# First block's maxima by pairs of key chunks over eight PSUM banks, and one-row reciprocals spread through HBM, in a kernel of attention and a non-local block

## The chip, the cores and the metric

The kernel runs on one NeuronCore of one Trainium2 chip. The metric is the device time of one execution in microseconds. Three runs of the kernel before gave 4115.18, 4115.48 and 4115.97 us; the median is 4115.48.

The engines are PE (TensorE, matrix products into PSUM), DVE (VectorE), ACT (ScalarE), POOL (GpSimd) and SP (SyncE, which here only issues DMAs). [...]

## The reference

The input x is 2 x 256 x 64 x 64. The first layer is self-attention over the 4096 pixels with 8 heads of 32 channels, the second a non-local block with pooled keys. Cut to what is computed:

```python
# layer 0
qkv = einsum('oc,bchw->bohw', w_qkv, x)
q, k, v = split(qkv, 3, axis=1)            # each b, 8 heads, 32, 4096
scores = einsum('bhdi,bhdj->bhij', q, k) / sqrt(32)
attn = softmax(scores, axis=-1)
out = einsum('bhij,bhdj->bhdi', attn, v)
x = einsum('oc,bchw->bohw', w_proj, out) + x
# layer 1
g = maxpool2(conv1x1(x, g_w, g_b))
theta = conv1x1(x[:, :64], theta_w, theta_b)
phi = maxpool2(conv1x1(x[:, 64:], phi_w, phi_b))
y = softmax(theta^T phi) @ g
x = batchnorm(conv1x1(y, W_w, W_b)) + x
```

Softmax subtracts the row's maximum before the exponential, and divides by the row's sum.

## The kernel before

Heads are taken four at a time; two batches with two such quads give four quads `n` = 0 to 3. In a quad the 4096 queries are eight blocks `i` of 512, so 32 blocks are attended one after another. Within a block the loop runs over 32 key tiles `j` of 128 keys. One step of it (L464 to L495) does, on PE, for each pair of heads, the subtraction of the row maxima (`subtract`, a small bfloat16 product, on even `j`) and the scores (`score`); on ACT the exponentials `p` (L481); on PE the product of the previous step's exponentials with v (`weigh`, into `w`); on DVE the addition of `w` into `num` (L401); and on POOL the sums of the exponentials for the denominator (`add`): the first pair of heads by an addition (L414), the second by an accumulating DMA of two tiles (L422).

The odd steps don't compute scores anew: keys of an odd chunk are stored as differences to the even chunk before (`kd` for the first four chunks of 512 keys, `last_kd` for the last four), and their product is added into the bank that still holds the even scores.

The row maxima of a block are needed before its attention, so they are found one block ahead, by the generator `maxima`, which the loop moves on by a step at a time (`advance(maxes)`). A step takes two heads. `plain` makes the product of 128 queries with 512 keys and takes its maximum over the keys on DVE (L249). `pair` finds the maximum over two chunks: the product with the differences, cut at zero by ACT (`over`, L256), and then the product with the even chunk, which DVE adds to `over` and reduces at once (L259). In the blocks after the first, heads 2 and 3 go mostly by `pair`, heads 0 and 1 by `plain`. All products of the maxima are in `scratch` tiles (four banks of pool `ps_m`); scores take tiles of two banks (pool `ps_s`, two of them). `scratch` also holds `w`, `den`, and k, q and v products during attention. Banks of a pool are given out in turn, and an allocation waits until the bank's last user is done.

Before attention starts, the opening loop (L701 to L708) makes k and v of quad 0, chunk by chunk, and q of two blocks; there the k, q and v products are in `ps_s`. Each is copied out by ACT (L187, L204). Between the halves of these products the maxima of the first block move on, all by `plain`: 128 products of 512 keys, 128 reductions. Then (L709 to L713) what remains of the first block is done, its maxima are negated into `neg` (L311), split into three bfloat16 terms on POOL, and the second block's maxima are begun.

A block's denominator is taken during the next block, by the generator `normalize`: at step 2 the last accumulating DMA, at step 6 the product with ones into `den` and ACT's copy of it into `r` (128x512; every head's row of 512 sums stands there 32 times), then eight reciprocals of 64 columns each, one a step (L451 to L455), and at the end the multiplication by POOL into `y` (L456). `issue_after(reduced.ins)` puts a reciprocal behind the maxima's last reduction on DVE. The two last blocks of the batches are normalized in `project`, halfway.

Loads of x are issued by SP (L88). In attention one tile holds x, so a load is issued as soon as the last product of the tile's previous content is done; steps 11, 19 and 27 make the next q, k and v from it.

The order on each engine is set by a scheduler that works from priorities and its own estimate of times, within the order of the data; each engine runs its instructions in that fixed order, and SP its DMA issues too.

Of the kernel before, what the change touches and what calls it, by code (L numbers as in the profile page):

```python
# [9 lines left out]
F32 = mybir.dt.float32  # L10
BF16 = mybir.dt.bfloat16
AF = mybir.ActivationFunctionType
# [5 lines left out]
HEADS, D = 8, 32  # L18
QH = 4
# [16 lines left out]
def conv_attention(  # L36
# [23 lines left out]


    ps_s = ctx.enter_context(tc.tile_pool(name="ps_s", bufs=2, space=bass.MemoryType.PSUM))
    ps_m = ctx.enter_context(tc.tile_pool(name="ps_m", bufs=4, space=bass.MemoryType.PSUM))

    def scores(name):
        return ps_s.tile([P, 2, NB], F32, tag="s", name=name)

    def scratch(name):
        return ps_m.tile([P, NB], F32, tag="m", name=name)
# [91 lines left out]
    def make(what, n, i):  # L161
        b, qd = QUAD[n]
        if held.get("x") != (b, i):
            held["x"] = (b, i)
            name = f"x_{what}_{n}_{i}"
            held["t"] = load_x(
                b, i, xs.tile([P, NC, NB], F32, tag="x", name=name) if attending else single(name)
            )
        xc = held["t"]
        name = f"{what}_{b}_{qd}_{i}"  # L170

        pq = scratch(name) if attending else scores(name)[:, 0, :]
        if what == "v":
            if i == 0:
                v[n] = qkv.tile([P, NJ, QH, D], F32, tag="v", name=f"v_{n}")
            for j in range(NB // P):
                for c in range(NC):
                    nc.tensor.matmul(  # L178
                        pq[:, bass.ts(j, P)],
                        xc[:, c, bass.ts(j, P)],  # L180
                        wv_sb[:, c, bass.ts(qd, P)],
                        start=(c == 0),
                        stop=(c == NC - 1),
                    )
                if j % 2 == 1:
                    yield
            nc.scalar.copy(v[n][:, bass.ts(i, NB // P)].rearrange("p j h d -> p (j h d)"), pq)  # L187
            return
        for c in range(NC):
            nc.tensor.matmul(  # L190
                pq,
                wqk_sb[:, c, qd, 0 if what == "q" else 1, :],
                xc[:, c, :],
                start=(c == 0),
                stop=(c == NC - 1),
            )
            yield
        if what == "q":
            to = q[n, i] = qkv.tile([P, NB], F32, tag="q", name=f"q_{n}_{i}", bufs=3)
        else:  # L200
            if i == 0:
                k[n] = qkv.tile([P, N], F32, tag="k", name=f"k_{n}")
            to = k[n][:, bass.ts(i, NB)]
        nc.scalar.copy(to, pq)  # L204
        if what == "k" and i == NI // 2 - 1:
            kd[n] = qkv.tile([P, NI // 4, NB], F32, tag="kd", name=f"kd_{n}")
            differences(n, 0, kd[n])

# [23 lines left out]
    part = const.tile([P, NB // P, QH, NI], F32, name="part")  # L232
    nc.vector.memset(part, LEAST)

    def product(n, i, g, h, keys):
        ps = scratch(f"ps_{n}_{i}_{g}_{h}")
        nc.tensor.matmul(  # L237
            ps,
            q[n, i][bass.ts(h, D), bass.ts(g, P)],
            keys[bass.ts(h, D), :],  # L240
            start=True,
            stop=True,
        )
        return ps

    def plain(n, i, g, h, j):
        nonlocal reduced
        ps = product(n, i, g, h, k[n][:, bass.ts(j, NB)])
        reduced = nc.vector.tensor_reduce(part[:, g, h, j : j + 1], ps, AX.X, ALU.max)  # L249

    def pair(n, i, g, h, jp):

        nonlocal reduced, cut
        ps = product(n, i, g, h, (kd[n] if jp < NI // 4 else last_kd)[:, jp % (NI // 4), :])
        over = work.tile([P, NB], F32, tag="over", name=f"over_{n}_{i}_{g}_{h}")
        cut = nc.scalar.activation(over, ps, AF.Relu)  # L256
        yield
        ps = product(n, i, g, h, k[n][:, bass.ts(2 * jp, NB)])
        reduced = nc.vector.tensor_tensor_reduce(  # L259
            out=ps,  # L260
            in0=ps,
            in1=over,
            scale=1.0,
            scalar=LEAST,
            op0=ALU.add,
            op1=ALU.max,
            accum_out=part[:, g, h, 2 * jp : 2 * jp + 1],
        )
        yield

    G = NB // P

    def of_head(n, i, h):

        chunks = 0 if h < 2 else NI // 2 if i == 0 else NI
        pairs = [(g, jp) for jp in range(chunks // 2) for g in range(G)]
        plains = [(g, j) for g in range(G) for j in range(chunks, NI)]
        if h == 3:  # L280
            if not plains:
                g, jp = pairs.pop()
                plains = [(g, 2 * jp), (g, 2 * jp + 1)]
            plain(n, i, plains[0][0], h, plains[0][1])
            plains = plains[1:]
            yield
        for x in pairs:
            yield from pair(n, i, x[0], h, x[1])
        for x in plains:
            plain(n, i, x[0], h, x[1])  # L290
            yield

    def maxima(n, i):
        if (n, i) == (0, 0):

            for j in range(NI):
                for g in range(G):
                    for two in (1, 0):
                        for h in (2 * two, 2 * two + 1):
                            plain(n, i, g, h, j)  # L300
                        yield
        else:
            heads = [of_head(n, i, h) for h in range(QH)]
            for step in range(G * NI):

                for two in ((2, 3) if step % 2 == 0 else (3, 2)), (0, 1):
                    for h in two:
                        next(heads[h])
                    yield
        neg = work.tile([P, NB // P, QH], F32, tag="neg", name=f"neg_{n}_{i}")  # L310
        nc.vector.tensor_reduce(neg, part, AX.X, ALU.max, negate=True)  # L311
        rows.append(negate(f"{n}_{i}", len(rows), neg))
        if i == 0:
            nc.vector.memset(part[:, :, 2:, :], LEAST)


# [9 lines left out]
    def advance(steps, n=1):  # L326
        for _ in range(n):
            next(steps, None)
# [12 lines left out]
    def attend(b, y):  # L341
# [82 lines left out]
        def normalize(blk):  # L424
            whole = [1, 2]
            if (blk.qd, blk.i) != (QUADS - 1, NI - 1):
                with tc.issue_after(added.ins):
                    nc.gpsimd.dma_start(out=blk.sums[1], in_=blk.sums[2], accum_op=ALU.add)
                whole = [1]
                yield  # L430
            den = scratch(f"den_{blk.name}")
            mine = [
                [blk.sums[0], *blk.last],
                [blk.sums[n][:, j] for j in range(2) for n in whole],
            ]
            for n in range(max(map(len, mine))):
                for h in range(QH):
                    those = mine[h // 2]
                    if n < len(those):
                        nc.tensor.matmul(  # L440
                            den[bass.ts(h, D), :],
                            ones[:, :D],
                            those[n][:, h % 2, :],
                            start=(n == 0),
                            stop=(n == len(those) - 1),
                        )
            r = work.tile([P, NB], F32, tag="r", name=f"r_{blk.name}", bufs=1)
            nc.scalar.copy(r, den)
            yield

            for c in range(8):  # L451
                cols = bass.ts(c, NB // 8)
                with tc.issue_after(reduced.ins):
                    nc.vector.reciprocal(r[:, cols], r[:, cols])
                yield  # L455
            nc.gpsimd.tensor_mul(y[:, blk.qd, bass.ts(blk.i, NB)], blk.num, r)  # L456

        waiting, normal = None, iter(())
        for qd in range(QUADS):
            for i in range(NI):  # L460
# [3 lines left out]
                for j in range(NJ):  # L464
# [24 lines left out]
                        advance(normal)  # L489
                    if j % 2 == 0:  # L490
                        make_rows()
                        if (i, j) == (0, NJ // 4):
                            differences(blk.n, 1, last_kd)
                    elif j % 8 == 3 and j > 8 and items:
                        advance(make(*items.pop(0)), 9)  # L495
# [202 lines left out]
    attending = False  # L698


    for i in range(NI + 1):  # L701
        items = [(what, 0, i) for what in "kqv" if i < (2 if what == "q" else NI)]
        for item in items:
            pieces = make(*item)
            for n in range(3):
                advance(pieces)
                if i > 0 and item[0] != "q" and n < 2:
                    advance(maxes, 2)  # L708
    advance(maxes, 8)  # L709
    advance(maxes)  # L710
    make_rows()
# [61 lines left out]
```

## Time and profile before

| What | Value |
|---|---|
| median of three runs | 4115.48 us |
| profiled execution, its own time | 4114.88 us |
| its span, first to last instruction | 4113.1 us |
| mean granted PE clock | 0.996 |
| opening stage, up to the first exponential | 125 us |
| attention of batch 0, one block, 463.00 to 570.55 us | 107.55 us |
| in that block, busy: DVE, ACT, POOL | 87.41, 80.83, 87.98 us |
| in that block, DMA share of 16 engines | 0.77 |
| one reciprocal of 128x64 on DVE | 543 ns |
| one maximum over a product, 128x512 | 686 ns, 0.61 us from one to the next |
| one cut of a product by ACT, 128x512 | 597 ns |
| one pair reduction on DVE, 128x512, and the read of its accumulator | 699 and 142 ns |

The page of the profile gives busy shares over the whole span; they mix an opening stage, two stages of attention of about 1725 us each, and two of projection and non-local block. So the stages are read one by one below. PE's busy time is modelled (its matmuls are pipelined), so the distance from one group of matmuls to the next says more than its busy share.

### The profile page before, as it was taken

How to read it: one execution, taken by the hardware profiler on the slowest of the kernel's cores; microseconds unless marked ns; L12 is line 12 of the kernel's file. 1: busy time of each engine (PE TensorE's matmuls, PEld its weight loads, DVE VectorE, ACT ScalarE, POOL GpSimd, SP SyncE). 2: the span in 40 equal slices, each digit the busy share in tenths (PEclk: the TensorE clock that was granted, in tenths of full speed). 3: DMA queues.
4: the chain of work that ended last, by engine and by line, in shares of the span. 5: the costliest groups of instructions: out<-in, count | busy, mean ns of one | idle time of the engine just before them, and what ended most of it. 6: DMA issues, size and time to landing. Idle time of an engine off the chain costs nothing.

```text
span 4113.1 us, 75018 instructions
## 1 busy us (share of the span) xinstructions
PE 4085.4 (99%) x29712; PEld 1539.1 (37%) x29712; DVE 3075.7 (75%) x5661; ACT 2647.4 (64%) x3264; POOL 2920.1 (71%) x1855
## 2 busy tenths in 40 slices
PE   9999999999999999999999999999999999999998
PEld 4433333333333333333333333333333333333333
DVE  7788888888888888884448888888888888883444
ACT  1677777776777777761137777777677777777111
POOL 0677887777877887780448878877788888889143
PEclk9899999999999999999999999999999999999999
DMA  1477777777777777781008777777777777778300
GB/s 58 102 157 158 158 157 157 155 163 156 156 157 156 161 157 162 162 171 45 21 21 165 158 161 160 155 157 158 158 163 157 156 159 157 151 155 172 80 16 26
DMA packets 98735, 560.70 MB, mean 136 GB/s; under 512 B 9552, under 2 KB 11344, under 8 KB 37200
## 3 DMA queue, kind: packets, MB, share of 16 engines
q0 software_dynamic: 68832, 501.25, 60.3%
q1 hardware_dynamic: 28288, 53.48, 4.5%
q8 instruction: 232, 3.80, 0.4%
q10 hardware_dynamic: 1264, 1.19, 0.1%
q14 instruction: 119, 0.97, 0.1%
HBM read 46.28 MB, written 8.39 MB: 13 GB/s over the span
## 4 chain that ended last, share of the span: by engine, by line
PE 97%; DVE 2%; DMA 0%; POOL 0%; issue 0%; ACT 0%; DVEq 0%; ACTq 0%; POOLq 0%
PE ps L237 31%; PE w L390 25%; PE s L366 18%; PE y L638 5%; PE s L378 5%; PE v L178 2%; PE k L190 2%; PE q L190 2%; PE den L440 1%; PE g L564 1%; DVE r L652 1%; PE f L606 1%; PE proj L510 1%; PE f L670 1%; PE tp L548 0%; PE tp L544 0%
## 5 line engine op out<-in xcount | busy, mean ns | idle before, releaser
L414 POOL TENSOR_TENSOR p<-p,p 128x1024 f32<-128x1024 f32 x960 | 2338.7, 2436 | 610.5 <-ACT p L481 490.8
L237 PE MATMUL ps<-k,q 32*128 32x512 f32 x6360 | 2206.5, 621 | 0.9 <-ACT over L256 0.6
L481 ACT ACTIVATE p<-s 128x1024 f32<-128x1024 f32 x2048 | 1990.7, 1024 | 114.7 <-PE ps L237 47.1
L249 DVE TENSOR_REDUCE part<-ps 128x1 f32<-128x512 f32 x2264 | 1453.1, 686 | 117.3 <-PE ps L237 74.7
L390 PE MATMUL w<-p,v 128*32 128x512 f32 x8192 | 1091.9, 605 | 0.0
L366 PE MATMUL s<-q,k 32*128 32x512 f32 x4096 | 1031.0, 595 | 0.0
L259 DVE CUSTOM_DVE_ANT_0 ps<-ps,over 128x512 f32<-128x512 f32 x916 | 639.8, 699 | 484.7 <-PE ps L237 255.0
L237 PEld LDWEIGHTS ps<-k,q 32*128 32x128 f32 x6360 | 830.6, 184 | 312.4 <-DVE num L401 103.3
L256 ACT ACTIVATE over<-ps 128x512 f32<-128x512 f32 x916 | 547.2, 597 | 615.0 <-PE ps L237 607.6
L401 DVE TENSOR_TENSOR num<-num,w 128x512 f32<-128x512 f32 x992 | 661.9, 667 | 80.3 <-PE w L390 77.7
L237 PE MATMUL ps<-kd,q 32*128 32x512 f32 x992 | 560.8, 645 | 0.0
L366 PE MATMUL s<-q,last_kd 32*128 32x512 f32 x2048 | 511.5, 614 | 0.0
L366 PE MATMUL s<-q,kd 32*128 32x512 f32 x2048 | 510.7, 615 | 0.6 <-ACT p L481 0.6
L237 PE MATMUL ps<-last_kd,q 32*128 32x512 f32 x840 | 470.6, 640 | 0.0
L390 PEld LDWEIGHTS w<-p,v 128*32 128x32 f32 x8192 | 161.5, 108 | 777.5 <-ACT over L256 685.6
L422 POOL DMA_DIRECT2D p<-p x448 | 388.8, 868 | 57.3 <-ACT p L481 53.5
L378 PE MATMUL s<-rows,ones_b 32*128 32x512 bf16 x2048 | 395.3, 380 | 0.2 <-ACT p L481 0.2
L366 PEld LDWEIGHTS s<-q,k 32*128 32x128 f32 x4096 | 366.7, 184 | 5.7 <-issue 1.4
L378 PEld LDWEIGHTS <-ones_b 32*128 32x128 bf16 x2048 | 128.6, 91 | 499.3 <-PE ps L237 209.6
L366 PEld LDWEIGHTS s<-q,kd 32*128 32x128 f32 x2048 | 174.3, 184 | 221.8 <-ACT p L481 192.5
L366 PEld LDWEIGHTS s<-q,last_kd 32*128 32x128 f32 x2048 | 173.9, 184 | 205.9 <-ACT p L481 186.7
L638 PE MATMUL y<-p,kv 128*128 128x512 f32 x512 | 240.0, 608 | 3.7 <-DVE r L652 3.7
(99 smaller groups left out, 2309.1 us busy)
## 6 DMA issues: line engine op xcount, KB each, us to landing
p<-p POOLq DMA_DIRECT2D x478, 1024.0 KB, 7.4
x_k<-in_x_dram SPq DMA_DIRECT2D x32, 512.0 KB, 4.1
x_q<-in_x_dram SPq DMA_DIRECT2D x30, 512.0 KB, 5.7
x_res<-in_x_dram SPq DMA_DIRECT2D x16, 512.0 KB, 8.5
out_dram<-z SPq DMA_DIRECT2D x16, 512.0 KB, 2.7
x_v<-in_x_dram SPq DMA_DIRECT2D x6, 512.0 KB, 4.4
wqk_sb<-in_wqk_dram ACTq DMA_DIRECT2D x1, 512.0 KB, 5.5
g<-in_gw_dram SPq DMA_DIRECT2D x2, 256.0 KB, 9.6
```

The source lines that it names most:

```text
L237: nc.tensor.matmul(ps, q[n, i][bass.ts(h, D), bass.ts(g, P)], keys[bass.ts(h, D), :], start=True, stop=True,)
L249: reduced = nc.vector.tensor_reduce(part[:, g, h, j : j + 1], ps, AX.X, ALU.max)
L256: cut = nc.scalar.activation(over, ps, AF.Relu)
L259: reduced = nc.vector.tensor_tensor_reduce(out=ps, in0=ps, in1=over, scale=1.0, scalar=LEAST, op0=ALU.add, op1=ALU.max, accum_out=part[:, ...
L366: nc.tensor.matmul(s[:, t, :], kj[bass.ts(h, D), :], q[blk.n, blk.i][bass.ts(h, D), :], start=False, stop=True, skip_group_check=j % 2 == 1,)
L378: nc.tensor.matmul(s[:, t, :], ones_b[bass.ts(h, D), :], rows[blk.rows][bass.ts(h, D), :], start=True, stop=False,)
L390: nc.tensor.matmul(w[bass.ts(h, D), :], v[blk.n][:, keys(j), h, :], p[h // 2][:, h % 2, :], start=True, stop=True,)
L401: nc.vector.tensor_add(blk.num, blk.num, w)
L414: added = nc.gpsimd.tensor_add(blk.sums[0], blk.sums[0], p[0])
L422: nc.gpsimd.dma_start(out=blk.sums[n], in_=two, accum_op=ALU.add)
L481: nc.scalar.activation(p[pair], s, AF.Exp, scale=scale)
L638: nc.tensor.matmul(acc[i][o], wg[:, 2 * t + j, bass.ts(o, P)], p[:, j, :], **edge)
```

## The change

Three things are changed together.

First block: its maxima are taken by pairs of chunks for all four heads. `first_block` makes, for a pair of chunks and a group of 128 queries, four products with the differences (two in scratch banks, two in the two banks of a scores tile), four cuts by ACT into a tile of the exponentials' pool, four products with the even chunk and four pair reductions. One step of the generator has four heads now. The opening loop has one round less and takes one such step between the halves of a k or v product from chunk 2 on, and the k, q and v products there go to scratch banks. The differences of quad 0 are made for each pair of chunks as soon as both are there, by a POOL operation of 128x512 each. As the first block leaves the odd slots of `part` at the least value, they are not reset for quad 0.

Reciprocals: the rows of `r` for the four heads, one for each, are written to HBM by a DMA, read back laid out over 128 partitions of 16 values (`few`), inverted in one operation on DVE, written to HBM, and copied by four DMAs to the 32 partitions of each head in `r`. The block normalized in the projection has one reciprocal of 128x512 instead.

Waits: five steps lie between the read back and the reciprocal in the written order, and five between the copies and the multiplication.

```diff
+    spare = ctx.enter_context(
+        tc.tile_pool(name="spare", bufs=2, space=bass.MemoryType.DRAM)
+    )
...
-        pq = scratch(name) if attending else scores(name)[:, 0, :]
+        pq = scratch(name)
...
-        if what == "k" and i == NI // 2 - 1:
+        if what == "k" and i % 2 == 1 and n == 0:
+            if i == 1:
+                kd[n] = qkv.tile([P, NI // 4, NB], F32, tag="kd", name=f"kd_{n}")
+            two = k[n][:, bass.ts(i // 2, 2 * NB)]
+            nc.gpsimd.tensor_sub(
+                (kd[n] if i < NI // 2 else last_kd)[:, i // 2 % (NI // 4), :],
+                two[:, NB:],
+                two[:, :NB],
+            )
+        elif what == "k" and i == NI // 2 - 1:
...
-    def product(n, i, g, h, keys):
-        ps = scratch(f"ps_{n}_{i}_{g}_{h}")
+    def product(n, i, g, h, keys, ps=None):
+        if ps is None:
+            ps = scratch(f"ps_{n}_{i}_{g}_{h}")
...
+    def first_block():
+        for jp in range(NI // 2):
+            for g in range(G):
+                over = double(f"over_{jp}_{g}").rearrange("p a b n -> p (a b) n")
+                for what in range(2):
+                    if what == 0:
+                        keys = (kd[0] if jp < NI // 4 else last_kd)[:, jp % (NI // 4), :]
+                    else:
+                        keys = k[0][:, bass.ts(2 * jp, NB)]
+                    s = scores(f"ps_{jp}_{g}_{what}")
+                    ps = [
+                        product(0, 0, g, h, keys, s[:, h - 2, :] if h >= 2 else None)
+                        for h in range(QH)
+                    ]
+                    for h in range(QH):
+                        if what == 0:
+                            nc.scalar.activation(over[:, h, :], ps[h], AF.Relu)
+                        else:
+                            joint(ps[h], over[:, h, :], g, h, jp)
+                    yield
...
-        chunks = 0 if h < 2 else NI // 2 if i == 0 else NI
+        chunks = 0 if h < 2 else NI // 2 if i == 0 and n > 0 else NI
...
         if (n, i) == (0, 0):
-            for j in range(NI):
-                for g in range(G):
-                    for two in (1, 0):
-                        for h in (2 * two, 2 * two + 1):
-                            plain(n, i, g, h, j)
-                        yield
+            yield from first_block()
...
-        if i == 0:
+        if i == 0 and n > 0:
             nc.vector.memset(part[:, :, 2:, :], LEAST)
...
-            for c in range(8):
-                cols = bass.ts(c, NB // 8)
+            if (blk.qd, blk.i) == (QUADS - 1, NI - 1):
+                nc.vector.reciprocal(r, r)
+            else:
+                flat = [spare.tile([QH, NB], F32, tag=f"flat{a}", name=f"flat{a}_{blk.name}") for a in range(2)]
+                few = work.tile([P, NB // D], F32, tag="few", name=f"few_{blk.name}")
+                nc.sync.dma_start(out=flat[0], in_=r[::D, :])
+                nc.sync.dma_start(out=few, in_=flat[0].rearrange("h (c e) -> (h c) e", c=D))
+                for _ in range(5):
+                    yield
                 with tc.issue_after(reduced.ins):
-                    nc.vector.reciprocal(r[:, cols], r[:, cols])
-                yield
+                    nc.vector.reciprocal(few, few)
+                nc.sync.dma_start(out=flat[1].rearrange("h (c e) -> (h c) e", c=D), in_=few)
+                for h in range(QH):
+                    nc.sync.dma_start(
+                        out=r[bass.ts(h, D), :], in_=flat[1][h : h + 1, :].broadcast_to([D, NB])
+                    )
+                for _ in range(5):
+                    yield
             nc.gpsimd.tensor_mul(y[:, blk.qd, bass.ts(blk.i, NB)], blk.num, r)
...
-                        if (i, j) == (0, NJ // 4):
+                        if (i, j) == (0, NJ // 4) and blk.n > 0:
                             differences(blk.n, 1, last_kd)
...
-    for i in range(NI + 1):
+    for i in range(NI):
         items = [(what, 0, i) for what in "kqv" if i < (2 if what == "q" else NI)]
         for item in items:
             pieces = make(*item)
             for n in range(3):
                 advance(pieces)
-                if i > 0 and item[0] != "q" and n < 2:
-                    advance(maxes, 2)
+                if i > 1 and item[0] != "q" and n < 2:
+                    advance(maxes)
```

`joint` is the pair reduction of before (L259 to L268) as a function of its own; `pair` calls it.

More of the change, by code (lines that the diff above doesn't have):

```diff
@@ L251, in pair @@
     def pair(n, i, g, h, jp):
-        nonlocal reduced, cut
+        nonlocal cut
         ps = product(n, i, g, h, (kd[n] if jp < NI // 4 else last_kd)[:, jp % (NI // 4), :])
@@ L257, in pair, with joint @@
         yield
-        ps = product(n, i, g, h, k[n][:, bass.ts(2 * jp, NB)])
+        joint(product(n, i, g, h, k[n][:, bass.ts(2 * jp, NB)]), over, g, h, jp)
+        yield
+    def joint(ps, over, g, h, jp):
+        nonlocal reduced
         reduced = nc.vector.tensor_tensor_reduce(
@@ L449, in normalize @@
             yield
-            for c in range(8):
-                cols = bass.ts(c, NB // 8)
-                with tc.issue_after(reduced.ins):
-                    nc.vector.reciprocal(r[:, cols], r[:, cols])
-                yield
+            if (blk.qd, blk.i) == (QUADS - 1, NI - 1):
[7 more added lines that the diff above has]
+                    yield
+                with tc.issue_after(reduced.ins):
+                    nc.vector.reciprocal(few, few)
[5 more added lines that the diff above has]
+                for _ in range(5):
+                    yield
             nc.gpsimd.tensor_mul(y[:, blk.qd, bass.ts(blk.i, NB)], blk.num, r)
```

## The prediction

> **What bounds the kernel now.** I read the page first, then the times of the matmuls `w` of one block of the attention loop, then the opening 125 us by windows, then POOL and the DMA queues.
>
> ```profile
> span 4113.1 us, 75018 instructions
> PE 4085.4 (99%) x29712; PEld 1539.1 (37%) x29712; DVE 3075.7 (75%) x5661; ACT 2647.4 (64%) x3264; POOL 2920.1 (71%) x1855
> PEclk9899999999999999999999999999999999999999
> PE 97%; DVE 2%; DMA 0%; POOL 0%; issue 0%; ACT 0%; DVEq 0%; ACTq 0%; POOLq 0%
> ```
>
> PE carries 97% of the chain of waits, but ends of matmuls are modelled, so "99% busy" doesn't say that PE never waits. The weigh matmuls `w` (L390), one group per key tile, are a clock for the loop. These are from the timeline of PE, in one block (start, length):
>
> ```profile
> 467.64 1.06 PE L390 MATMUL w<-p,v 128*32 128x512 f32 x8
> 471.22 1.07 PE L390 MATMUL w<-p,v 128*32 128x512 f32 x8
> 474.18 1.06 PE L390 MATMUL w<-p,v 128*32 128x512 f32 x8
> 477.72 1.07 PE L390 MATMUL w<-p,v 128*32 128x512 f32 x8
> 480.71 1.07 PE L390 MATMUL w<-p,v 128*32 128x512 f32 x8
> ...
> 498.83 1.06 PE L390 MATMUL w<-p,v 128*32 128x512 f32 x8
> 501.82 1.07 PE L390 MATMUL w<-p,v 128*32 128x512 f32 x8
> 504.96 1.06 PE L390 MATMUL w<-p,v 128*32 128x512 f32 x8
> 507.95 1.06 PE L390 MATMUL w<-p,v 128*32 128x512 f32 x8
> ...
> L454 DVE RECIPROCAL r<-r x256: 494/543/554, 253.9 to 3837.9; 128x64 f32<-128x64 f32 x128
> ```
>
> The reader is to see that the late steps take 2.99 and 3.14 us in turn, while steps with a reciprocal (key tiles 7 to 14) take 3.58, 2.96, 3.54, 2.99, then (after the step that also makes q) 3.40, 3.14, 3.40. So four of the eight 543 ns reciprocals delay PE by 0.41 to 0.45 us: DVE runs the addition into `num` after the reciprocal, and the scratch bank that it frees comes late. DVE is the bound of these steps, hidden under "PE".
>
> The opening stage, by windows (us, busy and count of PE, PEld, DVE, ACT, POOL, granted clock, DMA):
>
> ```profile
> 40.00:60.00 20.00, 20.00 (x94) 9.71 (x93) 16.22 (x28) 1.76 (x3) 2.35 (x1) 1.00 0.00 1
> 100.00:120.00 20.00, 20.00 (x57) 12.83 (x54) 15.93 (x29) 2.39 (x4) 1.22 (x5) 0.53 0.00 0
> ...
> 94.08 15.83 DVE L249 TENSOR_REDUCE part<-ps 128x1 f32<-128x512 f32 x24 [0.96 <-PE ps L237]
> ```
>
> DVE is the bound (81%), ACT is nearly empty, and PE's clock is halved near 101 to 125 us. The first block's maxima end with the reduction into `neg` at 109.94 us and attention starts near 121.5.
>
> [...]one halving lasts from about 2138.8 to 2142.3 us[...]. [...]reciprocal and addition into `num` always follow in the order written. [...]
>
> **The change, part by part.**
>
> (a) Reciprocals. Removed: 8 x 543 ns a block on DVE. Added in the place of the sixth: one of 128x16. From the rows 128x64 (543 ns) and 128x512 (3358 ns, L652) the slope is 6.28 ns an element and the intercept 141, so 0.24 us. Against 3.13 and 2.99 the excess over steps 7 to 14 is 0.45 - 0.03 + 0.42 + 0 + 0 + 0.41 + 0 + 0.41 = 1.66 us. A reciprocal of 0.54 costs 0.41, so 0.13 of it is covered; 0.24 costs 0.11. Gain 1.55 us a block. Thirty blocks are normalized inside the loop; the last of these lies in a block without maxima, whose steps show no excess. 29 x 1.55 = 45 us. Next late is PE's own 2.99 and 3.13, and I take these whole because the late steps of the same blocks, with the same other work, already run at that pace. Bounds: 22 us, if only half goes, to 48 us. The two blocks normalized in the projection get one reciprocal of 3.36 us for eight of 0.54: 1 us less, under 28 us of projection matmuls: nothing.
>
> (b) Seven DMAs more a block on SP: the lay-out (4 x 2 KB), the read back (128 x 64 B), the write (128 x 64 B), and four copies of 64 KB. `r` is copied by ACT at 250.73 us in the second block; with 0.37 us per SP issue and 3 to 4 us to landing (x loads of 512 KB take a median 4.1 to 5.7 with these queues; I take 3 for small ones), the row values are in `few` by 259, and the reciprocal stands at 271.9: 12 us of cover. SP's order puts the load of x for q ahead of the lay-out, and that for k (free when q's matmuls end at 268.6) ahead of the write, so no load is late. DMA bytes grow by 0.3 MB a block against 17. Nothing.
>
> (c) The multiply on POOL moves. In the instruction order of the new kernel it stands two additions earlier, straight behind the addition of key tile 13 and ahead of the accumulating DMA of tile 12. Before:
>
> ```profile
> 274.51 2.36 POOL L414 TENSOR_TENSOR p<-p,p 128x1024 f32<-128x1024 f32 x1 [0.82 <-ACT p L481]
> 276.82 0.86 POOL L422 DMA_DIRECT2D p<-p  x1
> 277.88 2.35 POOL L414 TENSOR_TENSOR p<-p,p 128x1024 f32<-128x1024 f32 x1 [0.20 <-ACT p L481]
> 280.20 1.27 POOL L456 TENSOR_TENSOR y<-num,r 128x512 f32<-128x512 f32 x1
> ...
> p<-p POOLq DMA_DIRECT2D x478, 1024.0 KB, 7.4
> x_k<-in_x_dram SPq DMA_DIRECT2D x32, 512.0 KB, 4.1
> ```
>
> So POOL can want `r` from 276.9. The chain: reciprocal done at 272.1, write lands at 275.2 (3 us), four issues of 0.37 to 276.7, last copy lands near 279.3. POOL waits about 2.4 us; behind it stand the accumulating DMA of 12 and the additions. That DMA starts at 281, not 276.8, and lands by 288.5. Its double buffer is next written by the exponential of tile 18, second pair, at 290.4; two reciprocals fewer bring that to 289.6. So it just fits: 1 us to spare, and POOL's idle time (0.94 us in two steps, 20%) takes up the rest. I take nothing, except in the last block where POOL is the bound (92% busy at 3700 to 3800): +2 us once. Bounds: 0 to 3 us in each of 29 blocks.
>
> (d) First block. DVE: 128 reductions of 0.61 us become 64 pair reductions of about 0.76 (0.70 and the read of the accumulator), 78 us to 49; ACT gains 64 cuts of 0.60, 38 us. But the banks decide. k and v products now use the four scratch banks in turn with the maxima: one for the product, two for the differences' heads 0 and 1, two for the even chunk's. The fifth falls on the bank of the k or v product itself, whose copy stands on ACT behind the four cuts. Each of the 12 passes (k and v of chunks 2 to 7) is thus a closed chain: bank free to PE 0.15 (a cut ends at 904.89, the next weigh starts at 905.03), four products 1.07, first half of the next k or v 1.06, four products 1.07, to ACT 0.08, four cuts 2.40, copy 0.59: 6.42 us, though PE has only 4.2 and DVE 3.0 of work. Passes start when chunk 1 is done, 20.9 us (chunk 0 to 14.6, then about 2.1 each for k, q, v): 20.9 + 12 x 6.42 = 98. The last four pairs are bound by DVE: 4 x 3.05 and 3 us to fill and drain, 113. Against 109.94: 3 us later, at full clock.
>
> (e) The clock. Count a matmul record of 128 rows as one and one of 32 rows as a quarter, 0.43 us each (four k records take 1.91). From 40 to 90 us the groups give 138 products, 20 k, 64 v of a quarter's length: (34.5 + 20 + 16) x 0.43 / 50 = 61% of the array, clock full. After 97.7 us only two products stand in every 1.22 us (two reductions): 35%, and the clock was halved. In the new chain the average is 3.44 / 6.42 = 54%, but in bunches: [...] at half clock the 3.2 us of PE in the chain double and the pass takes 9.6. Its dense stretch, first half, four products, second half, is 3.2 us, 6.4 at half clock[...]. I take half of the passes slow: 6 x 3.2 = 19 us. Bounds: 0, and all 12 with the tail, 41 us.
>
> Sum, on the profiled execution of 4114.88 us (span 4113.1 and 1.8 around it; 0.6 below the median): -45 + 3 + 19 + 2 = -21, which is 4094; against the median 4094.5. I say 4094.
>
> **Rivals.** A change within 0.2%, 8 us, is no change that can be told.
> - Forecast, clock swings in the opening: 4094, own range 4082 to 4105. Chance 0.45.
> - The clock stays full, or the bank chain is looser than I read it: -45 + 3 + 2, 4075. For it: the average of 54% is near the 61% that held. Against: the bunches. 0.15.
> - The clock locks at half through the opening: -45 + 3 + 41 + 2, 4116. For it: once halved before, it stayed so for 24 us of sparse work. Against: the denser stretch. 0.20.
> - Slower: the multiply waits too long for `r`. Place: POOL, behind tile 13. Price: each us beyond about 1 more than I reckon stalls an exponential in 29 blocks; slower than before from 0.9 us a block (21 + 8 over 29), and at 2 us 4152. For it: 64 B writes and a busy DMA (77%). Against: 1 us of room and POOL's idle time. 0.12.
> - Half of (a) only, because another release is late in these steps: 4116. Against: the late steps. 0.08.
>
> Faster: 0.44 + 0.15 + 0.04 + 0.02 = 0.65. Within 0.2%: 0.11 of the locked clock, 0.04 of the last case, 0.01: 0.16. Slower: 0.12 + 0.05 + 0.02 = 0.19. The range runs from the second case less its error in (a), 4070, to the locked clock with a little of POOL, 4124; of the chances about 0.13 lie outside.
>
> **What would show it.** Steps 7 to 14 at 2.99 and 3.13; in the opening, the maxima's products waiting for ACT's copy once a pass of 6.4 us, and the end of `neg`'s reduction near 132 us (113 at full clock, 155 if locked); granted clock under 1 between 25 and 110 us; POOL's multiply idle by 2 to 3 us before it, released by a DMA of `r`; no wait of ACT's exponentials for p<-p. I am wrong if passes take under 5.5 us, if steps 7 to 14 keep an excess over 0.5 us a block, or if exponentials wait for DMA.

## The result and the profile after

The changed kernel takes 4075.32 us (median of four runs, 4069.38 to 4079.79); the kernel before, run beside it, 4115.33. The ratio is 0.9902, with a 95% interval of 0.9885 to 0.9919: about 40 us, or 1%, less. The profiled execution took 4069.38 us, with a span of 4067.6; it is the fastest of the four, so its trace shows the small side of what the change loses.

The page of the changed kernel:

```profile
span 4067.6 us, 75418 instructions
PE 4022.1 (99%) x29712; PEld 1496.0 (37%) x29712; DVE 2951.2 (73%) x5436; ACT 2674.9 (66%) x3328; POOL 2925.4 (72%) x1857
PE 89%; DMA 6%; DVE 2%; POOL 1%; ACT 1%; issue 1%; SPq 0%; POOLq 0%; DVEq 0%; ACTq 0%
```

The time fell, and yet DMA now has 6% of the chain of waits, where it had 0%. So something was gained and something else was newly lost. The two have to be read in their stages.

**The opening.** The timeline of PE for two passes (start, length; a k or v product comes in two halves, with four products of the maxima, eight records, behind each):

```profile
20.16 1.14 PE L249 MATMUL ps<-kd,q 32*128 32x512 f32 x8
21.23 1.12 PE L192 MATMUL k<-x_k,wqk_sb 128*128 128x512 f32 x2
22.29 1.14 PE L249 MATMUL ps<-k,q 32*128 32x512 f32 x8
23.36 1.16 PE L180 MATMUL v<-wv_sb,x_k 128*128 128x128 f32 x8
24.45 1.14 PE L249 MATMUL ps<-kd,q 32*128 32x512 f32 x8
...
28.73 1.14 PE L249 MATMUL ps<-kd,q 32*128 32x512 f32 x8
```

From 20.16 to 24.45 and from there to 28.73: a pass takes 4.29 us, and PE has no gap in it. It isn't the closed chain of 6.42 us that the prediction saw. ACT's copy of k starts at 23.25, when the second set of products (22.29) has long been going. Then the windows around the end of the opening (us; PE, PEld, DVE, ACT, POOL; granted clock, DMA):

```profile
60.00:80.00 20.00, 18.44 (x116) 8.61 (x120) 15.11 (x43) 13.81 (x27) 1.27 (x1) 1.00 0.00 1
80.00:90.00 10.00, 8.87 (x41) 3.81 (x38) 9.39 (x24) 3.93 (x8) 1.22 (x5) 0.99 0.00 1
90.00:100.00 10.00, 10.00 (x37) 5.18 (x34) 5.07 (x11) 3.58 (x5) 0.00 (x0) 0.50 0.01 2
100.00:110.00 10.00, 9.77 (x83) 3.24 (x84) 7.84 (x15) 8.74 (x12) 5.05 (x3) 0.99 0.00 0
```

The granted clock is 1.00 through the passes, which end near 71 us, and halved (0.50) only from 90 to 100 us. The reduction into `neg` starts at 85.72 us (before: 109.94), the first exponential at 99.49 (before: 125.08). So 24.2 us come from the maxima, and 1.4 from the stretch between `neg` and the first exponential, 13.8 us instead of 15.1. That makes 25.6.

**The blocks.** The matmuls `w` of one block, from the step with `den` on (the first five):

```profile
332.97 1.06 PE L422 MATMUL w<-p,v 128*32 128x512 f32 x8
336.14 1.06 PE L422 MATMUL w<-p,v 128*32 128x512 f32 x8
339.09 1.06 PE L422 MATMUL w<-p,v 128*32 128x512 f32 x8
342.23 1.06 PE L422 MATMUL w<-p,v 128*32 128x512 f32 x8
345.22 1.06 PE L422 MATMUL w<-p,v 128*32 128x512 f32 x8
```

The steps of the block take 3.17, 2.95, 3.14, 2.99, then 5.05 (with q), 3.10, 3.13 and 2.99 us, where before they took 3.58, 2.96, 3.54, 2.99, 5.05, 3.40, 3.14 and 3.40: the delays by the reciprocals are gone but for about 0.1 us. A reciprocal of `few` takes 244 ns. But 25.6 in the opening and the predicted 45 in the blocks would be 71, and the spans differ by 45.5. The timeline of one block, SP, POOL, ACT and PE in turn, shows where the rest went:

```profile
454.41 0.38 SPq L91 DMA_DIRECT2D x_k<-in_x_dram  x1
457.92 0.33 SPq L495 DMA_DIRECT2D flat<-few  x1
463.67 1.72 SPq L497 DMA_DIRECT2D r<-flat  x4
...
460.31 2.36 POOL L446 TENSOR_TENSOR p<-p,p 128x1024 f32<-128x1024 f32 x1 [0.83 <-ACT p L527]
467.11 1.27 POOL L502 TENSOR_TENSOR y<-num,r 128x512 f32<-128x512 f32 x1 [4.44 <-DVE part L261]
468.33 0.87 POOL L454 DMA_DIRECT2D p<-p  x1
...
474.45 1.02 ACT L527 ACTIVATE p<-s 128x1024 f32<-128x1024 f32 x1
476.86 1.02 ACT L527 ACTIVATE p<-s 128x1024 f32<-128x1024 f32 x1 [1.39 <-DMA p<-p]
...
471.80 1.06 PE L422 MATMUL w<-p,v 128*32 128x512 f32 x8
474.93 1.06 PE L422 MATMUL w<-p,v 128*32 128x512 f32 x8
479.00 1.06 PE L422 MATMUL w<-p,v 128*32 128x512 f32 x8
```

SP can issue the four copies only 5.75 us after the write of `few`, when that has landed. POOL ends the addition of key tile 13 at 462.67 and stands idle for 4.44 us until `r` is there. (DVE's `part` is named as the releaser, but that instruction has nothing to do with `r`; in 18 other blocks the copies are named. Over all 30 blocks the mean wait is 4.9 us.) Only then, at 468.33, goes the accumulating DMA of tile 12, and the exponential of tile 18, which writes the same buffer, waits 1.39 us for it. The step of `weigh` becomes 4.07 us instead of 2.99. Over the whole run, by the list of waits (sum in us, how often, longest):

```profile
POOL y L502 <- DMA r<-flat: 89.7, 18, 6.0
POOL y L502 <- DVE part L261: 45.7, 10, 5.5
ACT p L527 <- DMA p<-p: 23.7, 22, 3.7
```

Before, exponentials waited 2.5 us in all for `p<-p`. The 21 us more are most of the 25 that are missing.

### The profile page after: what moved, and what is told of

The parts are those of the page before. It is cut to its first block, busy times and chain, and to the rows that moved or that the text cites. A ratio compares the mean times of both kernels' runs of the same rounds, so it can differ in the third digit from the quotient of the medians.

```text
span 4067.6 us, 75418 instructions
## 1 busy us (share of the span) xinstructions
PE 4022.1 (99%) x29712; PEld 1496.0 (37%) x29712; DVE 2951.2 (73%) x5436; ACT 2674.9 (66%) x3328; POOL 2925.4 (72%) x1857
## 4 chain that ended last, share of the span: by engine, by line
PE 89%; DMA 6%; DVE 2%; POOL 1%; ACT 1%; issue 1%; SPq 0%; POOLq 0%; DVEq 0%; ACTq 0%
PE ps L249 27%; PE w L422 22%; PE s L398 16%; PE y L684 5%; PE s L410 5%; DMA p<-p 4%; PE v L180 2%; PE k L192 2%; PE q L192 2%; PE g L610 1%; PE den L472 1%; DVE r L698 1%; DMA flat<-few 1%; PE f L652 1%; PE f L716 1%; PE proj L556 1%
## 5 line engine op out<-in xcount | busy, mean ns | idle before, releaser
L446 POOL TENSOR_TENSOR p<-p,p 128x1024 f32<-128x1024 f32 x960 | 2364.8, 2463 | 446.4 <-ACT p L527 313.6
L249 PE MATMUL ps<-k,q 32*128 32x512 f32 x6232 | 2123.4, 618 | 3.4 <-DVE part L275 2.1
L261 DVE TENSOR_REDUCE part<-ps 128x1 f32<-128x512 f32 x2136 | 1374.6, 686 | 117.2 <-PE ps L249 73.9
L275 DVE CUSTOM_DVE_ANT_0 ps<-ps,over 128x512 f32<-128x512 f32 x980 | 683.7, 700 | 554.2 <-PE ps L249 299.2
L398 PE MATMUL s<-q,k 32*128 32x512 f32 x4096 | 1019.8, 593 | 0.0
L268 ACT ACTIVATE over<-ps 128x512 f32<-128x512 f32 x916 | 547.4, 598 | 557.7 <-PE ps L249 550.1
L249 PEld LDWEIGHTS ps<-k,q 32*128 32x128 f32 x6232 | 786.2, 183 | 263.7 <-DVE num L433 83.1
L433 DVE TENSOR_TENSOR num<-num,w 128x512 f32<-128x512 f32 x992 | 671.9, 677 | 81.5 <-PE w L422 78.2
L249 PE MATMUL ps<-last_kd,q 32*128 32x512 f32 x904 | 482.9, 639 | 0.0
```

Of the source, the lines that this page charges most:

```text
L249: nc.tensor.matmul(ps, q[n, i][bass.ts(h, D), bass.ts(g, P)], keys[bass.ts(h, D), :], start=True, stop=True,)
L275: reduced = nc.vector.tensor_tensor_reduce(out=ps, in0=ps, in1=over, scale=1.0, scalar=LEAST, op0=ALU.add, op1=ALU.max, accum_out=part[:, ...
L398: nc.tensor.matmul(s[:, t, :], kj[bass.ts(h, D), :], q[blk.n, blk.i][bass.ts(h, D), :], start=False, stop=True, skip_group_check=j % 2 == 1,)
L433: nc.vector.tensor_add(blk.num, blk.num, w)
L446: added = nc.gpsimd.tensor_add(blk.sums[0], blk.sums[0], p[0])
```

## Experiments

**Each part alone.** The first kernel has the first block of the change and the reciprocals of before, the second the reciprocals of the change and the opening of before.

The end of `normalize` in the first kernel, against the changed one:

```diff
-            if (blk.qd, blk.i) == (QUADS - 1, NI - 1):
-                nc.vector.reciprocal(r, r)
-            else:
...
+            for c in range(8):
+                cols = bass.ts(c, NB // 8)
                 with tc.issue_after(reduced.ins):
-                    nc.vector.reciprocal(few, few)
...
+                    nc.vector.reciprocal(r[:, cols], r[:, cols])
+                yield
```

> Only the first block's part of the change; the eight reciprocals of 128x64 and the multiply stand as before. Theory (the two parts add, and the first block's is worth what the opening shows, the first exponential at 99.5 us for 125.1): 25.6 us less than before, 4089.7, between 4088 and 4092. Rival (the earlier start is partly given back in the blocks, which would explain why the whole change brought 40 and not 71 us): above 4097.

Measured: 4089.32 us (4089.11 to 4092.25), 25.5 less than the 4114.82 of before; ratio 0.9940, 0.9927 to 0.9952. The opening's gain is kept whole.

> Only the reciprocals' part, with the opening as before. Theory (45 us gained on DVE in 29 blocks, and 20 to 30 us of it given back by POOL's multiply that waits for r): 4092 to 4102, with POOL idle before the multiply in most blocks and exponentials waiting for the accumulating DMA. Rival (the reciprocals' part is worth its whole 45 us and the loss comes with the opening's part): 4068 to 4073.

Measured: 4105.52 us (4097.21 to 4112.08), only 9.3 less; ratio 0.9974, 0.9967 to 0.9982. It is 3.5 us above the theory's window, and far from the rival's. In its trace the exponentials wait 39.9 us for `p<-p` (30 times), more than in the changed kernel; but this trace is of an execution 6.6 us above its median, that of the changed kernel of one 5.9 us below. So the loss belongs to the reciprocals' part, and its size varies: 15 runs of this kernel spread over 15 us, five of the first over 3.

**The multiply two additions later.**

```diff
-                for _ in range(5):
+                for _ in range(3):
                     yield
-            nc.gpsimd.tensor_mul(y[:, blk.qd, bass.ts(blk.i, NB)], blk.num, r)
+            with tc.issue_after(added.ins):
+                nc.gpsimd.tensor_mul(y[:, blk.qd, bass.ts(blk.i, NB)], blk.num, r)
```

> The changed kernel with POOL's multiply put back behind the addition of key tile 15, where the kernel before had it, two additions later than in the changed one; nothing else moves. Theory (the wait of the multiply for r is what gives back the 25 us): r lands at about 9.2 us after the write is issued and the multiply's turn then comes later than that, so no idle time before it, no exponential waits for the accumulating DMA, 4043 to 4052. Rival (the small DMAs as such[...] slow the accumulating DMAs, wherever the multiply stands): 4065 or more, with exponentials still waiting for p<-p.

Measured: 4046.33 us (4045.84 to 4047.84), ratio 0.9833, 0.9820 to 0.9847. The 29 us come back: exponentials wait 4.3 us in all for `p<-p`. But the expectation was wrong in one thing: POOL still waits for `r`, as its timeline shows.

```profile
465.79 2.36 POOL L446 TENSOR_TENSOR p<-p,p 128x1024 f32<-128x1024 f32 x1 [0.68 <-ACT p L528]
470.59 1.28 POOL L503 TENSOR_TENSOR y<-num,r 128x512 f32<-128x512 f32 x1 [2.44 <-DMA r<-flat]
471.82 0.86 POOL L454 DMA_DIRECT2D p<-p  x1
```

From the issue of the copies to a multiply that waited it is now 6.5 to 8.9 us, where the changed kernel has a median of 3.5: the accumulating DMA of tile 12 goes out ahead of the copies, and they land later. The waits, 28 with a mean of 3.0 us, look free here. With the multiply behind tile 17 even these are gone:

> The changed kernel with the multiply behind the addition of tile 17, where r has landed. Theory (behind tile 15 the wait of 2.3 to 3.9 us was already free): within 3 us of the variant behind tile 15, 4043 to 4048, POOL without idle time for r. Rival (those waits still cost something): 4036 to 4042.

Measured: 4046.15 us (4045.20 to 4046.75), no idle time ahead of the multiply, and the same time to 0.2 us. Behind tile 15 a wait of 3 us cost nothing.

**The multiply behind the accumulating DMA.** Is it the DMA that the wait holds back, or the additions?

```diff
+                    summed = nc.gpsimd.dma_start(out=blk.sums[n], in_=two, accum_op=ALU.add)
...
-                for _ in range(5):
-                    yield
+                yield
+            with tc.issue_after(summed.ins):
+                nc.gpsimd.tensor_mul(y[:, blk.qd, bass.ts(blk.i, NB)], blk.num, r)
```

> The changed kernel with POOL's multiply one place later: behind the accumulating DMA of key tile 12 and still ahead of the addition of tile 14. POOL then waits for r as long as before, but the DMA has been issued. Theory (the wait costs because the accumulating DMA of tile 12 stands behind it, and the exponential of tile 18 writes its buffer): POOL still idle by 4 to 5 us ahead of the multiply, exponentials waiting for p<-p under 8 us in all, 4044 to 4052. Rival (the idle time delays the additions, and these the exponentials): 4062 to 4075.

Measured: 4122.95 us (4113.76 to 4131.77), slower than before; ratio 1.0019, 1.0013 to 1.0026. Both theories missed it: the exponentials wait 74.1 us in all for `p<-p` (47 times). SP and POOL in one block:

```profile
465.44 0.33 SPq L495 DMA_DIRECT2D flat<-few  x1
472.36 3.66 SPq L497 DMA_DIRECT2D r<-flat  x4
...
470.14 0.86 POOL L454 DMA_DIRECT2D p<-p  x1
478.83 1.28 POOL L502 TENSOR_TENSOR y<-num,r 128x512 f32<-128x512 f32 x1 [7.83 <-DMA r<-flat]
480.08 4.78 POOL L446 TENSOR_TENSOR p<-p,p 128x1024 f32<-128x1024 f32 x2
484.80 0.87 POOL L454 DMA_DIRECT2D p<-p  x1
```

The 1 MB of tile 12 (470.14) now runs against the copies (from 472.36): they need 6.5 us, and up to 9.3 in other blocks, where the changed kernel needs 3.5. Their issue alone takes SP 3.66 us in place of 1.72. The wait grows from a mean of 4.9 to 8.2 us, and what stands behind it, two additions and the accumulating DMA of tile 14, is late instead. The long steps are now those of tiles 20 and 21 (5.89 and 4.64 us in the second block), not 18. So the multiply of the changed kernel, by holding the DMA of tile 12 back, had kept its own copies from running against it. The question that the run was to settle, DMA or additions, stays open, because the wait did not keep its length.

**Is the write slow because its rows have 64 B?** The values in 16 rows of 512 B, by the same DMAs:

```diff
-                few = work.tile([P, NB // D], F32, tag="few", name=f"few_{blk.name}")
+                few = work.tile([4 * QH, NB // 4], F32, tag="few", name=f"few_{blk.name}", bufs=1)
...
-                nc.sync.dma_start(out=flat[1].rearrange("h (c e) -> (h c) e", c=D), in_=few)
+                nc.sync.dma_start(out=flat[1].rearrange("h (c e) -> (h c) e", c=4), in_=few)
```

The read back is laid out the same way. To make room, `few` and two small tiles of other parts have one buffer less.

> The changed kernel with the values laid out over 16 partitions of 128 instead of 128 of 16, so that the write to HBM and the read back have rows of 512 B instead of 64 B; the order is the same (two small tiles of other parts have one buffer less, to make room). In the changed kernel the copies are issued a median 5.8 us after the write. Theory (the write waits in the queues behind the 1 MB accumulating DMA and the 512 KB load issued 3.4 and 3.5 us before it; in the last block, without these, it took 1.6 us): still 5 us or more, POOL's wait for r as long, 4072 to 4086, the reciprocal of 128 elements costing up to 12 us more. Rival (128 descriptors of 64 B are what is slow): 3.5 us or less, and the exponentials' waits go.

Measured: 4081.80 us (4080.37 to 4084.23), inside the theory's window; the mean wait for `r` is 4.9 us, as in the changed kernel. Of this variant and then of the changed kernel, the same block on SP, and of the changed kernel two blocks more:

```profile
348.89 0.39 SPq L91 DMA_DIRECT2D x_k<-in_x_dram  x1
353.09 0.30 SPq L495 DMA_DIRECT2D flat<-few  x1
358.34 1.69 SPq L497 DMA_DIRECT2D r<-flat  x4
```

```profile
348.23 0.38 SPq L91 DMA_DIRECT2D x_k<-in_x_dram  x1
351.75 0.34 SPq L495 DMA_DIRECT2D flat<-few  x1
357.73 1.72 SPq L497 DMA_DIRECT2D r<-flat  x4
...
3511.40 0.34 SPq L495 DMA_DIRECT2D flat<-few  x1
3516.21 1.71 SPq L497 DMA_DIRECT2D r<-flat  x4
...
3705.40 0.34 SPq L495 DMA_DIRECT2D flat<-few  x1
3707.01 1.71 SPq L497 DMA_DIRECT2D r<-flat  x4
```

With 512 B rows the write has landed 9.45 us after the load of x was issued, with 64 B rows 9.50, though the write of 512 B rows was itself issued 0.7 us later (by the prediction's line, 141 ns and 6.28 ns an element, an estimated 0.9 us for the reciprocal of 128 elements where that of 16 took 0.24). The landing went with the DMAs ahead, not with the row length. In the last block, where no load was made and the last accumulating DMA was 8.2 us old, the same 64 B write took 1.61 us (with 512 B rows 1.53).

Of the two, the accumulating DMA weighs more. The block at 3511 us has no load in the 107 us before its write, but an accumulating DMA issued 3.35 us before it, as in the other blocks: 4.81 us, against a median of 5.8 with both. In the block after it, again without a load, that DMA was only 1.44 us old, and the write took 6.50 us. In both the write landed about 8 us after the accumulating DMA was issued, close to the 7.5 us that such a DMA takes itself (median); with the load as well it was 8.8 to 10.6 us. What the load adds, some 1 us by these two blocks, is not settled.

**The reciprocal three steps earlier,** the multiply left where the change put it:

```diff
-                for _ in range(5):
+                for _ in range(2):
                     yield
                 with tc.issue_after(reduced.ins):
                     nc.vector.reciprocal(few, few)
...
-                for _ in range(5):
+                for _ in range(4):
                     yield
-            nc.gpsimd.tensor_mul(y[:, blk.qd, bass.ts(blk.i, NB)], blk.num, r)
+            with tc.issue_after(added.ins):
+                nc.gpsimd.tensor_mul(y[:, blk.qd, bass.ts(blk.i, NB)], blk.num, r)
```

> The changed kernel with the reciprocal three steps earlier, so that the write and the four copies are issued some 9 us earlier and ahead of the load of x for k; the multiply stays where the change put it, behind tile 13 and ahead of the accumulating DMA of tile 12. Theory (it is the late r and not the multiply's place that costs): no idle time for r, exponentials waiting under 8 us in all, 4044 to 4052. Rival (the place itself costs, 1.3 us of POOL ahead of that DMA): 4058 to 4075.

Measured: 4044.75 us (4043.59 to 4045.68), ratio 0.9830, 0.9817 to 0.9844. Ahead of the load of x, and 4.5 us behind an accumulating DMA instead of 3.4, the write lands in 2.6 to 4.6 us in the first six blocks; the run doesn't separate these two. In the last block, with no load but 1.9 us behind an accumulating DMA, it took 6.93 us. POOL's timeline:

```profile
355.71 2.36 POOL L446 TENSOR_TENSOR p<-p,p 128x1024 f32<-128x1024 f32 x1 [0.82 <-ACT p L528]
358.02 1.29 POOL L503 TENSOR_TENSOR y<-num,r 128x512 f32<-128x512 f32 x1
359.24 0.88 POOL L454 DMA_DIRECT2D p<-p  x1
```

The multiply follows the addition at once, the accumulating DMA goes out on time, and the exponentials wait 2.1 us in all for `p<-p`. The place costs nothing; the late `r` did. The median is 1.4 us below that with the multiply behind tile 17, but the ranges overlap.

**Banks strictly in turn.** Why were the passes of the opening 4.29 us?

```diff
     def scratch(name):
-        return ps_m.tile([P, NB], F32, tag="m", name=name)
+        turn[0] += 1
+        return ps_m.tile([P, NB], F32, tag=f"m{turn[0] % 4}", name=name, bufs=1)
```

> The changed kernel with the four scratch banks given out strictly in turn (four tiles of one bank each, taken by a counter), in the whole kernel. Theory (the prediction's chain through ACT's copy of k or v was right for banks in turn, and fell only because the scheduler gives whichever bank it takes to be free): a k or v pass of the opening takes 6.2 to 6.6 us, the reduction into neg ends near 110 us, and PE's clock is halved somewhere between 25 and 110 us. Rival (the copy isn't the limit even in turn): passes stay at 4.3 us, neg near 86 us. The time of the whole says little, as the blocks' banks change too.

Measured: the opening's timeline of PE.

```profile
29.60 1.14 PE L252 MATMUL ps<-k,q 32*128 32x512 f32 x6 [0.47 <-ACT v L192]
...
32.79 1.13 PE L195 MATMUL k<-x_k,wqk_sb 128*128 128x512 f32 x2
33.84 1.12 PE L252 MATMUL ps<-k,q 32*128 32x512 f32 x2
35.47 1.13 PE L252 MATMUL ps<-k,q 32*128 32x512 f32 x6 [0.51 <-ACT k L209]
36.53 1.16 PE L183 MATMUL v<-wv_sb,x_k 128*128 128x128 f32 x8
```

A pass takes 5.87 us, a little under the expected 6.2 to 6.6, and the product that would take the k bank waits for ACT's copy, as predicted. So the predicted chain exists, but only with banks in turn. `neg` starts at 104.17 us, not near 110. The halving came before 110 us in the letter only: the clock is 1.00 in every window of 20 us from 20 to 100 us, that is through the passes, and 0.83 from 100 to 110. (The whole took 4153.08 us in one run; the blocks' banks change too.)

**The stretch after neg.** On top of the kernel with the earlier reciprocal, two of seven steps of the second block's maxima stay ahead of attention, and five go into its first steps:

```diff
-    advance(maxes, 2 * LEAD - 1)
+    advance(maxes, 2)
...
+                    if blk.rows == 0 and 1 <= j <= 2 * LEAD - 3:
+                        advance(maxes)
```

> The variant with the earlier reciprocal (4044.75 us), and the opening's last stretch shortened: of the seven steps of the second block's maxima that stand ahead of the first block's attention, two stay there and five go into key tiles 1 to 5 of that block, one to each. In the changed kernel 13.8 us lie between neg (85.7 us) and the first exponential (99.5), 10.2 of them at half clock, and the product pt waits in PE's order behind these products. Theory (five steps of about two products each at half clock, about 1.06 us a step, go; in the block they cost about half at full clock): neg to the first exponential 8 to 10 us, 4040 to 4043. Rival[...]: 12 us or more there, 4044 or more.

Measured: 4044.66 us (4044.05 to 4047.74), the same as without. `neg` to the first exponential shrank to 7.0 us (84.83 to 91.85) from 14.9 in the kernel that it was built on, and the granted clock from 80 to 100 us rose to 0.91 from 0.68. But the first steps of the block became 4.2 to 4.6 us, where steps without such work take 3.0 to 3.2, and nearly all of the gain was given back there. Neither side had foreseen that: the work was only moved.

## Why the prediction was right, and where it was wrong

The forecast of 4094 was 19 us too high: on the right side and inside the whole range of 4070 to 4124, but under the 4082 to 4105 of its own case. Its sum was right in its largest term. Of the others, the opening, (d) and (e), was put 47 us too high and the multiply, (c), about 29 us too low. That the result lay so near is luck: these errors cancelled in part.

(a) Reciprocals, -45: right. Between the kernel with only the first block's part (4089.32) and two of those in which `r` costs no time the difference is 43.0 (4046.33) or 44.6 us (4044.75). The reading of the steps, 1.55 us a block in 29 blocks, stands, and so does the estimate of 0.24 us for the reciprocal.

(b) The small DMAs on their own, nothing: right. The two best kernels issue them all and lose nothing to them. That holds only while nobody waits for them.

(c) The multiply, 0 to 3 us a block, taken as nothing: the mechanism right to the tile, one term mis-sized. The text has the write landing after 3 us; it took a median 5.8. With that, POOL's wait became 4.9 us (mean) instead of 2.4. The slack was sized well: 2.4 and "1 us to spare" make 3.4, and the runs show 4.9 costing (4075.32 - 4044.75) / 29 = 1.05 us a block, and 3.0 free, though two additions later. So what the prediction called its slower rival took place, at about 30 us in all. The term failed for a reason that its own text held: it has the load for k ahead of the write on SP, and asked only whether the load would be late, not what the load, and the accumulating DMA issued with it, do to the write. It put a small DMA at 3 us, below the loads' median of 4.1. Yet the trace before has a small DMA among large ones: the load of the parameters, 7.0 KB in rows of 56 B, took 7.7 us there beside the large loads of the opening. The runs show 1.61 us for this write where nothing recent was ahead, and a median of 5.8 where it was. The landings go with what was ahead (9.45 and 9.50 us after the load, though one write was issued 0.7 us later than the other); by what mechanism, no run here shows.

(d) First block, +3: wrong, and this is the step that failed. That "k and v products now use the four scratch banks in turn" isn't so, nor is the sentence of the kernel's description above. The second set of products starts at 22.29 us, before k's copy does (23.25), so it isn't waiting for that bank: the fifth tile got another one. (That the scheduler gives whichever bank it takes to be free is my reading; the traces don't show which bank each tile got.) The closed chain of 6.42 us a pass doesn't exist; PE has no gap, and the pass is the 4.29 us of its own work, which the prediction had at 4.2. `neg` came at 85.72 us for 113, and (d) and (e) together were -25.5 in place of +22. Pairs, the two more banks and the place of the k, q and v products came in one part, and no run separates what each brought. With banks forced in turn the pass was 5.87 us for a predicted 6.42; most of the rest is ACT, whose four cuts took 2.06 us, not 2.40.

(e) The clock, +19: wrong too, and not only because of (d). With passes of 4.29 us it stayed at 1.00, but with passes of 5.87 us it did as well. That the bunches would bring it down was the author's estimate: in the run with banks in turn, the sparse stretch from the end of k's second half (33.92) to the next half (36.53) is 2.6 us, and passes with such stretches left the clock at 1.00. How long or how sparse a stretch has to be before the clock is halved, no run shows. The average of 59% (the prediction's 3.44 us of array work, itself an estimate, in 5.87) served better here, close to the 61%, counted in the same way, that held in the kernel before. As in that kernel (0.50 from 101 to 125 us), the halving came only behind the dense part (0.50 from 90 to 100 us in the changed kernel).

The second case of the prediction, "the bank chain is looser than I read it", at 4075, gives the measured number, but for a wrong reason: it took the opening as 3 us slower and the multiply's wait as free. Two errors of about 28 us each cancelled in it.

Of the signs named for the forecast, the steps at 2.99 and 3.13 us came true, and POOL's idle time ahead of the multiply, though 4.9 us for 2 to 3. Two of those named against it came true as well: passes under 5.5 us, and exponentials that wait for DMA. By its own signs, then, the account was wrong, however near the number. One price among the rivals is a slip: (21 + 8) / 29 is 1.0 us a block, not 0.9.

## What to carry to other kernels

A small DMA can take as long as the large ones ahead of it: here the same 8 KB took 1.6 us with little ahead of it, 4.8 and 6.5 behind a fresh 1 MB accumulating DMA, and a median of 5.8 behind that and a load. When a result goes through HBM and somebody waits for it, look at what the queues carry from its issue to its landing, and issue it where they are clear, or early enough to wait them out. If a wait can't be avoided on an engine that starts nothing else meanwhile (POOL, in the 4.44 us ahead of its multiply), ask what stands behind it, and which DMA that is: here a wait of 3 us was free, and one of 5 two additions earlier cost 1 us a block, and letting the large DMA go first made it worse, as it ran against the very copies that were waited for. Before a chain of buffers is counted as closed, see in the built program which buffer each tile really gets, or in a trace whether anything waits for it.

## What was not expected of the hardware

The landing of the same 8 KB write, in 128 rows of 64 B, ran from 1.6 us (no load or fresh accumulating DMA ahead) to 7.3 us in the changed kernel. No cost of the 64 B rows against 512 B could be seen beside the traffic (landed 9.50 and 9.45 us after the load), and with little of it the two row lengths took 1.61 and 1.53 us.

Runs of kernels in which something waits at cost for such a DMA spread more: 10 us in four runs of the changed kernel, 15 us in 15 runs and 18 us in 21 runs of the two with the most waiting. The variants without such a wait spread over 1.6 to 3.7 us in four or five runs, but so did the one with 512 B rows (3.9 us in four), which waits too, and more runs find more of a range. A wide spread is a hint that a landing time is on the path, no proof.
